# The last batch's first experts: dense after attention, or sparse beside the linear attention

## The chip, the cores and the metric

The kernel runs on one core of one Trainium2 chip. A time is the device time of one execution in microseconds (us); the time of a kernel is the median of its runs. Engines are named as the profile names them: PE (TensorE, matmuls), PEld (its weight loads), DVE (VectorE), ACT (ScalarE), POOL (GpSimd), SP (SyncE, which here issues most transfers). L412 is line 412 of the kernel before.

## What is computed

Four batches of 1024 tokens, each token a row of 128 numbers, pass through four steps, each added to its input:

```python
x = x + attention(x)          # 16 heads of 64, causal, softmax; then @ Wo + bo
x = x + moe(layernorm(x))     # softmax over 32 experts, the best two are used
x = x + linear(layernorm(x))  # 16 heads of 8
x = x + moe(layernorm(x))     # the same experts again
...
def moe(x):                   # expert: a 128x128 matrix
    gates, ids = top_k(softmax(x @ router_w.T), 2)
    return sum(gates[:, j] * (x @ expert_weights[ids[:, j]]) for j in range(2))
...
def linear(x):                # per head; softplus features
    qf = softplus(q) * (sigmoid(g) + 1e-6);  kf = softplus(k)
    kv_cum = cumsum(kf[:, :, None] * v[:, None, :]);  z_cum = cumsum(kf)
    return (qf @ kv_cum) / (qf . z_cum + 1e-6) @ Wo.T
```

The cumulative sums run over the 1024 tokens of a batch. A token's first mixture of experts needs only its own row, so a batch may be in one step while another is in the next.

## The kernel before, in words

All activations stay in one tile `x_sb` of 32 blocks of 128 tokens, eight blocks a batch (`NB = 8`, `NT = 32`). Every step adds into it.

**Attention (L478 to L836).** Its instructions go to the engines in the order in which the code writes them (`tc.manual_schedule()`). For each batch and each pair of heads it goes through eight blocks of queries; `project_out` (L710, L715) multiplies by `Wo` and adds to `x_sb`. At the end of each slot `beside(k)` (L735) runs one or three entries of the list `queue` and one step of the first generator in `sides`.

**Sparse experts, `experts(b, ...)` (L206 to L474).** A generator; each `yield` ends a step. Statistics of eight blocks on DVE (L218); `rstd` and `nb` on POOL (L224); the normed rows on ACT (L240), their transposes on PE, the router's matmul (L248); Exp, the best two, counts (POOL, and PE with a triangle of ones), a list of experts that need another tile (`inc`, `which`) and the place of each token's two rows (`u`, `pos`, `row`). Then come 16 **scatters** (L366): POOL issues an indirect transfer of 128 weighted rows to their places in DRAM and a small memset behind it. The **stream** handles 47 tiles of 128 rows in 12 groups: SP loads rows (L402) and weights (L407, L414), PE transposes (L433), ACT copies (L435), PE multiplies (L422), DVE copies (L427), SP stores (L428). At last 16 **gathers** (L441), indirect transfers issued on POOL: in the first mixture they add straight into `x_sb`; in the second (`came` given) they land in tiles that DVE adds (L468, L473), and SP stores the batch. The scatters and gathers are put into `queue` and run one by one. `passing` lets only one stream run at a time. The small tiles of a run live in a `Room`, and `room.busy` keeps a second run out until the scatters are done.

Before, batches 0, 1 and 2 go through it beside the attention of the batch after each. When attention ends, a loop `while sides or queue` steps until batch 2's gathers are issued.

**Dense experts, `moe(...)` (L849 to L927).** For four blocks at a time (`q`): norm, router, the best two as 32 weights of which 30 are zero; then for each block eight calls of 128x512, four experts each, against all weights held in `we_sb` (L899). Three of eight results are weighted by ACT (L907) and added by POOL (L921 to L924), five are weighted and added by DVE (L914). Its instructions are not in a written order: a scheduler places them. Before, batch 3's first mixture is `moe("f", ...)` (L1043), and so is batch 3's second, `moe("s", ...)` (L1188), at the end of the kernel.

**Linear attention.** `prepare(t, pool)` (L959 to L1034) makes the features of four blocks: statistics (DVE, L966), `rstd` and `nb` (POOL, L971, L974), normed rows (ACT, L980), transposes, projections `pj` (PE, L998), their pieces (ACT, L1002 to L1005), softplus by Exp and Ln (ACT, L1013 to L1021), `ln` and `kq` (POOL, L1027). Before, `prepare(0)` and `prepare(1)` are placed inside the dense stage by `early` (L1036). The constants `tri` (POOL, L944) and `rest` (DVE, L950) stand ahead of it. Then, in a written order again, the loop over blocks `u` (0 to 35, four for the drain): `cumulate` (PE with `tri`, L1077), `products` of the next block (`kv`, POOL, L1059, and a copy on ACT), `outputs` (DVE multiplies the sums with q, L1097), `carry` (PE with `rest`, L1085), `finish` in four steps (L1103 to L1126: a sum, a quotient, a transpose, the output matrix, the residual). Three times in each `u`, `ahead(third)` steps the running `prepare`s (one starts once `12 * started - 26 <= third`) and `beside()` runs one entry of `queue` and one step of every generator of `sides`. The second experts of batches 0, 1 and 2 begin at u = 11, 19 and 27 through `waiting`, in the rooms a, b, a. What is left of them runs between the calls of `moe("s")`.

Of the kernel before, what the change touches and what calls it, by code (L numbers as in the profile page):

```python
# [11 lines left out]
ALU = mybir.AluOpType  # L12
AX = mybir.AxisListType
PSUM = bass.MemoryType.PSUM

P = 128
# [4 lines left out]
def hybrid_kernel(  # L21
# [17 lines left out]
    nc = tc.nc  # L39
    B, N, D = x.shape  # L40
    NB = N // P
    NT = B * NB
# [141 lines left out]
    room = Room(xo, "a")  # L184
# [289 lines left out]
        nc.sync.dma_start(out=out_v[b], in_=x_sb[:, c0 : c0 + NB, :])  # L474


    last = [None]
    with attn as ph:  # L478

        ph.enter_context(tc.manual_schedule())  # L480
# [6 lines left out]
        ps_1 = ph.enter_context(tc.tile_pool(name="ps_1", bufs=3, space=PSUM))  # L487
# [217 lines left out]
        def project_out(b, prs, oTs):  # L705

            for c in range(NB):
                pw = ps_1.tile([P, 512], F32, tag="ps1", name=f"pw_{b}_{c}")
                for i, pr in enumerate(prs):
                    nc.tensor.matmul(  # L710
                        pw[:, :P], oTs[i][:, c * P : (c + 1) * P], wo_sb[:, pr, :],
                        start=(i == 0), stop=(i == len(prs) - 1),
                    )
                xs = x_sb[:, b * NB + c, :]
                last[0] = nc.vector.tensor_tensor(xs, pw[:, :P], xs, ALU.add)  # L715
                yield

        pairs = [(b, pr) for b in range(B) for pr in range(NPAIR)]
# [1 line left out]
        AHEAD = (1, 1, 0, 0, 1, 2, 1, 0)  # L720
# [3 lines left out]
        cur, ahead = project(0, 0)  # L724
# [4 lines left out]
        outs, norms = iter(()), iter(())  # L729
        pend, oTs = None, []  # L730
        HALF = 2
        sides, queue = [], []

        def beside(k):

            for _ in range(3 if k % 2 else 1):
                if queue:
                    queue.pop(0)()
            while sides:
                if next(sides[0], "end") != "end":  # L740
                    break
                sides.pop(0)

        def piece():
            while weighing:
# [50 lines left out]
        for i, (b, pr) in enumerate(pairs):  # L796
            nm = f"{b}_{pr}"
            qT, kT, va = cur
            oT = otp.tile([P, N], F32, tag="oT", name=f"oT_{nm}")
            oTs.append(oT)  # L800
            ahead = iter(())
            if pr == NPAIR - 3 and b + 1 < B:
                norms = normed(b + 1)
            if i + 1 < len(pairs):
                nxt, ahead = project(*pairs[i + 1])
            twos = {}
            for k, ib in enumerate(ORDER):
                two = ib // 2
                if two not in twos:
                    twos[two] = [  # L810
                        ptp.tile([P, 2 * two + 2, 256], F32, tag=f"pT{two}_{h}", name=f"pT_{nm}_{two}_{h}")
                        for h in range(2)
                    ]
                u = Unit(nm, ib, qT, kT, twos[two], ib % 2 * P)
                if k == 5 and pend and pr % HALF == 0:
                    outs = project_out(*pend)
                    pend = None
                if k == 6 and pr == 0 and b > 0:
                    sides.append(experts(b - 1, f"{b - 1}", [ps_1], queue, room))
# [21 lines left out]
    xp = ctx.enter_context(tc.tile_pool(name="xp", bufs=1))  # L841
    came = ctx.enter_context(tc.tile_pool(name="came", bufs=3))
# [87 lines left out]

    lin = ExitStack()
    lw = lin.enter_context(tc.tile_pool(name="lw", bufs=1))
    lb = lin.enter_context(tc.tile_pool(name="lb", bufs=3))
    G = 4
    NE = LD + 1
    PARTS = 3
# [17 lines left out]
    feats = {}  # L957
# [87 lines left out]
    with lin as ph:  # L1045

        ph.enter_context(tc.manual_schedule())
        lp = ph.enter_context(tc.tile_pool(name="lp", bufs=3))
        ps_c = ph.enter_context(tc.tile_pool(name="ps_c", bufs=1, space=PSUM))
        ps_n = ph.enter_context(tc.tile_pool(name="ps_n", bufs=1, space=PSUM))  # L1050
        ps_1 = ph.enter_context(tc.tile_pool(name="ps_l", bufs=4, space=PSUM))
        AHEAD = 26

        def products(u):
# [77 lines left out]
        banks = [ps_1]  # L1132
# [11 lines left out]
        def beside():  # L1144

            if queue:
                queue.pop(0)()
            while waiting and not rooms[waiting[0] % 2].busy:
                b = waiting.pop(0)
                r = rooms[b % 2]  # L1150
                sides.append(experts(b, f"s{b}", banks, queue, r, came))
            for e in list(sides):
                if next(e, "end") == "end":
                    sides.remove(e)

        kv = products(0)
        ends = []
        for u in range(NT + 4):
            if u % NB == 3 and NB < u < NT:
                waiting.append(u // NB - 1)  # L1160
            if u < NT:
                cumulate(u, kv)
                nkv = products(u + 1) if u + 1 < NT else None
                ahead(3 * u)
                m = outputs(u)
            beside()
# [12 lines left out]
            beside()  # L1179

    def rest(pool):

# [40 lines left out]
```

## Time and profile before

| | |
|---|---|
| median of three runs | 2074.32 us (2070.86 to 2074.47) |
| profiled execution, its own time | 2072.33 us |
| its span | 2070.6 us |
| mean granted TensorE clock | 0.953 |
| busy PE / DVE / ACT / POOL | 1846.8 / 1411.0 / 1209.8 / 1168.8 us |
| attention's last matmul, dense stage "f" | 1507.7, then to 1612.4 us |
| first cumulation (u = 0) | 1612.42 us |
| u = 11, u = 16 | 1679.5, 1718.1 us |
| first call of dense "s" | 1876.10 us |

Busy time is the time in which an engine's own instructions run. A line of the timeline gives start, busy time, engine, source line, operation and tiles, and in brackets the idle time of the engine just ahead and what ended it. A line by stretches gives the busy time of each engine in a part of the span; an engine near the stretch's length is its bound, and if none is, the waits tell what it is.

### The profile page before, as it was taken

The page shows a single profiled execution, that of the slowest core. Times are in us where ns is not written, and L with a number is a line of the kernel's source. Part 1 is how long each engine was busy: PE and PEld are TensorE (multiplying, and loading weights), DVE is VectorE, ACT ScalarE, POOL GpSimd, SP SyncE. Part 2 cuts the span into 40 slices and gives each one's busy share as a digit, 9 for nine tenths or more (in the row PEclk, how much of TensorE's full clock was granted, in tenths as well). Part 3 has the DMA queues.
Part 4 walks back from the last instruction along what each step waited for, and adds up shares of the span by engine and source line. Part 5 has one row for each costly group of instructions (what it writes and reads, how often), then busy time and mean ns, then how long its engine had stood idle before and what let it go on. Part 6 is the DMA issues. An engine that isn't in the chain of part 4 may idle for free.

```text
span 2070.6 us, 33623 instructions
## 1 busy us (share of the span) xinstructions
PE 1846.8 (89%) x10100; PEld 1061.6 (51%) x10100; DVE 1411.0 (68%) x4147; ACT 1209.8 (58%) x3777; POOL 1168.8 (56%) x2174
## 2 busy tenths in 40 slices
PE   5999999999999999999999999999668888785765
PEld 2555555555555655555565555556433444463442
DVE  4677776776777677778767778776356677673525
ACT  3766666676676666766666676675345465422312
POOL 3444444444675486457646745683644675967625
PEclk9999999999999999999999999999879998887868
DMA  7000000000003310000231000014210000054651
GB/s 210 1 1 1 1 1 1 1 1 1 1 15 91 92 20 6 1 1 10 67 111 26 11 1 1 3 56 117 45 45 1 1 0 1 18 169 125 191 155 43
DMA packets 151443, 85.22 MB, mean 41 GB/s; under 512 B 8000, under 2 KB 148704, under 8 KB 151136
## 3 DMA queue, kind: packets, MB, share of 16 engines
q1 hardware_dynamic: 139456, 68.91, 11.8%
q0 software_dynamic: 11520, 12.60, 2.8%
q8 instruction: 82, 1.34, 0.3%
q10 hardware_dynamic: 288, 1.57, 0.2%
q14 instruction: 97, 0.79, 0.1%
HBM read 50.02 MB, written 33.03 MB: 40 GB/s over the span
## 4 chain that ended last, share of the span: by engine, by line
PE 61%; ACT 12%; POOL 11%; DVE 10%; issue 4%; SPq 1%; DMA 1%; another core or an unknown queue 1%; ACTq 0%; POOLq 0%; DVEq 0%
PE s L589 18%; PE po L695 10%; PE pt L678 10%; DVE nmx L598 5%; ACT p L623 3%; PE pw L710 3%; PE pk L538 3%; PE pe_f L899 3%; ACT pT L682 2%; POOL x_sb L441 2%; PE cum L1077 2%; PE cum L1085 2%; PE pv L552 2%; PE pe L422 2%; POOL p L665 1%
## 5 line engine op out<-in xcount | busy, mean ns | idle before, releaser
L598 DVE TENSOR_REDUCE nmx<-s 128x2 f32<-128x1024 f32 x512 | 604.5, 1220 | 216.3 <-PE s L589 208.4
L623 ACT ACTIVATE p<-s,nmx 128x512 f32<-128x512 f32 (+3 forms) x640 | 360.7, 575 | 310.1 <-DVE nmx L598 276.7
L589 PE MATMUL s<-kT,qT 64*128 64x512 f32 x2048 | 516.8, 618 | 7.5 <-ACT p L623 4.1
L665 POOL TENSOR_SCALAR p<-p,f,ri 128x512 f32<-128x512 f32 (+3 forms) x768 | 502.8, 670 | 0.7 <-PE s L589 0.4
L678 PEld LDWEIGHTS pt<-ident,p 128*128 128x128 f32 x2304 | 249.3, 141 | 218.0 <-issue 96.6
L678 PE MATMUL pt<-ident,p 128*128 128x128 f32 x2304 | 335.5, 281 | 23.9 <-POOL rs L643 7.0
L682 ACT COPY pT<-pt 128x512 f32<-128x512 f32 (+3 forms) x768 | 323.8, 509 | 13.9 <-PE pt L678 9.5
L647 POOL TENSOR_TENSOR rs<-rs,f 128x2 f32<-128x2 f32 x256 | 51.8, 203 | 438.8 <-ACT f L614 409.3
L695 PE MATMUL po<-pT,va 128*64 128x256 f32 (+1 forms) x2560 | 291.1, 365 | 0.6 <-DVE oT L702 0.6
L589 PEld LDWEIGHTS s<-kT,qT 64*128 64x128 f32 x2048 | 173.0, 185 | 194.8 <-issue 94.9
L628 ACT ACTIVATE p<-s,nmx 128x128 f32<-128x128 f32 x512 | 180.3, 365 | 107.4 <-DVE nmx L598 103.1
L695 PEld LDWEIGHTS po<-pT,va 128*64 128x64 f32 x2560 | 167.0, 136 | 97.2 <-issue 32.4
L636 DVE SCALAR_TENSOR_TENSOR p<-p,qtri 128x128 f32<-128x128 f32 x512 | 145.9, 312 | 6.7 <-ACT p L628 3.3
L643 POOL TENSOR_TENSOR rs<-rs 128x2 f32<-128x2 f32 x192 | 43.8, 228 | 185.7 <-DVE ri L656 185.7
L623 ACT ACTIVATION_READ_ACCUMULATOR p<-s,nmx 128x1 f32 x640 | 138.9, 217 | 0.0
L710 PE MATMUL pw<-wo_sb,oT 128*128 128x128 f32 x512 | 85.5, 292 | 21.9 <-DVE x_sb L715 21.1
L710 PEld LDWEIGHTS pw<-wo_sb,oT 128*128 128x128 f32 x512 | 69.3, 192 | 49.4 <-DVE x_sb L715 21.3
L422 PE MATMUL pe_s<-we_s,xsT_s 128*128 128x128 f32 x282 | 53.0, 333 | 42.7 <-ACT xsT_s L435 20.7
L715 DVE TENSOR_TENSOR x_sb<-pw,x_sb 128x128 f32<-128x128 f32 x128 | 37.1, 290 | 79.3 <-PE pw L710 78.4
L899 PE MATMUL pe_s<-we_sb,xnT_ms 128*128 128x512 f32 x128 | 71.9, 689 | 15.5 <-DVE x_sb L468 5.8
L441 POOL DMA_INDIRECT x_sb<-ys_d,row x48 | 75.8, 1579 | 12.3 <-issue 12.0
L1077 PE MATMUL cum<-kv,tri 128*128 128x384 f32 x192 | 76.1, 537 | 7.2 <-POOL kv L1059 7.0
(330 smaller groups left out, 2764.4 us busy)
## 6 DMA issues: line engine op xcount, KB each, us to landing
xs<-xs_d SPq DMA_DIRECT2D x33, 256.0 KB
ys_d<-ys SPq DMA_DIRECT2D x33, 256.0 KB
xs_s<-xs_d SPq DMA_DIRECT2D x33, 256.0 KB
ys_d<-ys_s SPq DMA_DIRECT2D x33, 256.0 KB
we<-_ffn_expert_weights_dram SPq DMA_DIRECT2D x24, 256.0 KB
we_s<-_ffn_expert_weights_dram SPq DMA_DIRECT2D x24, 256.0 KB
xs_d<-zero SPq DMA_DIRECT2D x2, 3008.0 KB
we<-_ffn_expert_weights_dram SPq DMA_DIRECT2D x45, 64.0 KB
```

What stands on the lines that cost most here:

```text
L589: nc.tensor.matmul(st[:, h, :], self.qT[rows, self.ib * P : (self.ib + 1) * P], self.kT[rows, j * 512 : (j + 1) * 512], start=True, stop=True,
L598: nc.vector.tensor_reduce(self.nmx[:, i, :], self.s[i], AX.X, ALU.max, negate=True)
L623: nc.scalar.activation(self.p[h][:, at : at + m * P], self.s[i][:, h, : m * P], AF.Exp, bias=bias, accum_out=self.rs[:, i, h : h + 1],)
L628: nc.scalar.activation(self.p[h][:, at + m * P : at + (m + 1) * P], self.s[i][:, h, m * P : (m + 1) * P], AF.Exp, bias=bias,)
L636: nc.vector.scalar_tensor_tensor(d, d, 1.0, qtri, ALU.mult, ALU.mult, accum_out=self.rs[:, 2, h : h + 1])
L665: nc.gpsimd.tensor_scalar(w, w, self.f[:, i, h : h + 1], self.ri[:, h : h + 1], ALU.mult, ALU.mult,)
L678: nc.tensor.transpose(pt[:, c * P : (c + 1) * P], self.p[h][:, (g + c) * P : (g + c + 1) * P], ident,)
L682: nc.scalar.copy(self.pTs[h][:, g : g + m, self.col : self.col + P], pt[:, : m * P].rearrange("p (c i) -> p c i", c=m),)
L695: nc.tensor.matmul(po[h * DH : (h + 1) * DH, c0:256], va[:, jb, h, :], pTs[h][:, jb, c0:], start=(jb == 0), stop=(jb == n - 1),)
L710: nc.tensor.matmul(pw[:, :P], oTs[i][:, c * P : (c + 1) * P], wo_sb[:, pr, :], start=(i == 0), stop=(i == len(prs) - 1),)
L899: nc.tensor.matmul(pe, xnT[:, c * P : (c + 1) * P], we_sb[:, 4 * g : 4 * g + 4, :].rearrange("p e d -> p (e d)"), start=True, stop=True,)
L1077: nc.tensor.matmul(sums[i][:, : EP * P], tri, part(kv, i), start=(u % NB == 0), stop=True, skip_group_check=True,)
```

## The change

The last batch's first mixture goes through `experts` too. It is started in the second step of attention's last `project_out`, and there is no loop that drains it: its steps go on inside the linear stage. The dense stage "f" with `early` is gone, and `prepare(0)` and `prepare(1)` are in the written order: 26 calls of `ahead` stand ahead of the first `products`. One `manual_schedule` now reaches from attention's start to the linear loop's end. `beside()` is called inside `ahead()`, three times in each `u`, and more if the features of the next block are not yet there. `prepare(6)`, the first of batch 3, is held until batch 3's experts are done. The rooms change places. The pools that come after attention take `reuse_waits="tile"`: a tile waits for those that used its own memory, not for all of the pool that was there.

```diff
+    order = ExitStack()
+    order.enter_context(tc.manual_schedule())
+    sides, queue = [], []
...
-            while sides:
-                if next(sides[0], "end") != "end":
-                    break
-                sides.pop(0)
+            for e in list(sides):
+                if next(e, "end") == "end":
+                    sides.remove(e)
...
         for _ in project_out(*pend):
+            if k == 1:
+                assert not room.busy
+                sides.append(experts(B - 1, f"{B - 1}", banks, queue, room))
+                final = sides[-1]
             beside(k)
             k += 1
-        while sides or queue:
-            beside(k)
-            k += 1
...
-    late = ctx.enter_context(tc.tile_pool(name="late", bufs=1))
+    late = ctx.enter_context(tc.tile_pool(name="late", bufs=1, reuse_waits="tile"))
...
-    def early(q, pool):
-
-        if q >= NT // 4 - 2:
-            with tc.issue_after(getattr(last[0], "ins", last[0])):
-                for _ in prepare(q - (NT // 4 - 2), pool):
-                    pass
-
-    moe("f", False, NT // 4 - 2, early)
...
-        started, running = 2, []
+        started, running = 0, []
...
+            while waiting and not rooms[(waiting[0] + 1) % 2].busy:
+                b = waiting.pop(0)
+                r = rooms[(b + 1) % 2]
+                sides.append(experts(b, f"s{b}", banks, queue, r, came))
...
             while started < NT // G and 3 * G * started - AHEAD <= third:
+                if G * started // NB == B - 1 and final in sides:
+                    break
                 running.append(prepare(started, ps_1))
                 started += 1
...
+            beside()
+
+        for third in range(-AHEAD, 0):
+            ahead(third)
         kv = products(0)
         ends = []
         for u in range(NT + 4):
+            while u + 1 < NT and (u + 1) // G not in feats:
+                ahead(3 * u)
             if u % NB == 3 and NB < u < NT:
                 waiting.append(u // NB - 1)
             if u < NT:
                 cumulate(u, kv)
                 nkv = products(u + 1) if u + 1 < NT else None
-                ahead(3 * u)
+            ahead(3 * u)
+            if u < NT:
                 m = outputs(u)
-            beside()
...
             ahead(3 * u + 1)
-            beside()
...
             ahead(3 * u + 2)
-            beside()
+    order.close()
```

The same argument stands on the pools `xp`, `came`, `lw`, `lb`, `lp`, `ps_c`, `ps_n` and `ps_l`.

More of the change, by code (lines that the diff above doesn't have):

```diff
@@ L474, in experts @@
         nc.sync.dma_start(out=out_v[b], in_=x_sb[:, c0 : c0 + NB, :])
-    last = [None]
+    order = ExitStack()
+    order.enter_context(tc.manual_schedule())
+    sides, queue = [], []
+    banks = [None]
     with attn as ph:
-        ph.enter_context(tc.manual_schedule())
         xnp = ph.enter_context(tc.tile_pool(name="xnpa", bufs=2))
@@ L714, in project_out @@
                 xs = x_sb[:, b * NB + c, :]
-                last[0] = nc.vector.tensor_tensor(xs, pw[:, :P], xs, ALU.add)
+                nc.vector.tensor_tensor(xs, pw[:, :P], xs, ALU.add)
                 yield
@@ L731, in hybrid_kernel @@
         HALF = 2
-        sides, queue = [], []
+        banks[0] = ps_1
         def beside(k):
@@ L818, in hybrid_kernel @@
                 if k == 6 and pr == 0 and b > 0:
-                    sides.append(experts(b - 1, f"{b - 1}", [ps_1], queue, room))
+                    sides.append(experts(b - 1, f"{b - 1}", banks, queue, room))
                 slot(u, (nm, ib - 1, twos[two], va, oT), k)
@@ L934, in hybrid_kernel @@
     lin = ExitStack()
-    lw = lin.enter_context(tc.tile_pool(name="lw", bufs=1))
-    lb = lin.enter_context(tc.tile_pool(name="lb", bufs=3))
+    lw = lin.enter_context(tc.tile_pool(name="lw", bufs=1, reuse_waits="tile"))
+    lb = lin.enter_context(tc.tile_pool(name="lb", bufs=3, reuse_waits="tile"))
     G = 4
@@ L1034, in prepare @@
         feats[t] = (kq, va)
-    def early(q, pool):
-        if q >= NT // 4 - 2:
-            with tc.issue_after(getattr(last[0], "ins", last[0])):
-                for _ in prepare(q - (NT // 4 - 2), pool):
-                    pass
-    moe("f", False, NT // 4 - 2, early)
-    with lin as ph:
[L1047 to L1051, printed above, removed]
+    with lin as ph:
+        lp = ph.enter_context(tc.tile_pool(name="lp", bufs=3, reuse_waits="tile"))
+        ps_c = ph.enter_context(tc.tile_pool(name="ps_c", bufs=1, space=PSUM, reuse_waits="tile"))
+        ps_n = ph.enter_context(tc.tile_pool(name="ps_n", bufs=1, space=PSUM, reuse_waits="tile"))
+        ps_1 = ph.enter_context(tc.tile_pool(name="ps_l", bufs=4, space=PSUM, reuse_waits="tile"))
         AHEAD = 26
@@ L1127, in finish, with beside @@
             yield
-        started, running = 2, []
+        started, running = 0, []
         waiting = []
         rooms = [room, Room(xp, "b")]
-        banks = [ps_1]
+        banks[0] = ps_1
+        def beside():
+            if queue:
+                queue.pop(0)()
+            while waiting and not rooms[(waiting[0] + 1) % 2].busy:
+                b = waiting.pop(0)
+                r = rooms[(b + 1) % 2]
+                sides.append(experts(b, f"s{b}", banks, queue, r, came))
+            for e in list(sides):
+                if next(e, "end") == "end":
+                    sides.remove(e)
         def ahead(third):
@@ L1142, in ahead @@
                     running.remove(r)
[L1144 to L1154, printed above, removed]
+            beside()
+        for third in range(-AHEAD, 0):
+            ahead(third)
         kv = products(0)
```

4 lines of the change are left out of this document (2 added, 2 removed).

## The prediction

> **What bounds the kernel now.** I read the page's busy shares and 40 slices first. TensorE is busy 97 to 98% of every stretch from 100 us to 1450 us (busy time by stretches), so the attention stage is TensorE's and the change leaves it alone. What the change touches lies after it, so the next view is busy time by stretches, cut where the timeline shows a stage begin: the end of attention, the dense experts "f", u = 0 to 10 of the linear loop, u = 11 to 15, u = 16 to 19, u = 20 to 30, and the tail. The columns are the stretch, its length, busy time with instruction count of PE, PEld, DVE, ACT and POOL, the granted TensorE clock, DMA share and GB/s.
>
> ```profile
> 1474.90:1507.70 32.80, 11.02 (x88) 8.63 (x86) 4.17 (x20) 1.64 (x4) 25.59 (x19) 0.71 0.27 32
> 1507.70:1612.40 104.70, 79.07 (x176) 34.98 (x176) 67.57 (x251) 55.98 (x159) 51.34 (x61) 0.86 0.08 21
> 1612.40:1679.50 67.10, 62.86 (x191) 35.17 (x192) 50.12 (x106) 37.20 (x96) 43.53 (x35) 0.93 0.00 0
> 1679.50:1718.10 38.60, 31.40 (x107) 18.49 (x105) 27.13 (x75) 25.28 (x57) 20.74 (x18) 0.90 0.00 1
> 1760.00:1820.00 60.00, 41.29 (x120) 24.04 (x121) 38.71 (x101) 25.39 (x68) 54.89 (x65) 0.83 0.05 18
> ```
>
> The reader is to see four things. Attention's last 33 us belong to POOL (25.6 of 32.8). The dense stage costs 104.7 us. With nothing beside it the linear loop is TensorE's: 62.86 of 67.10, 94%. Where the experts of another batch run beside it (last line, a part of u = 20 to 30), POOL is what is full: 54.89 of 60, 91.5%.
>
> The timeline shows how the stages hang together (start, busy time, instruction; in brackets the idle time before it and what ended it):
>
> ```profile
> 1502.95 1.56 POOL L441 DMA_INDIRECT x_sb<-ys_d,row  x1 [0.30 <-issue]
> ...
> 1505.13 0.23 DVE L950 TENSOR_SCALAR rest<-tri 128x128 f32<-128x128 f32 x1 [21.59 <-POOL tri L945]
> 1505.61 2.08 PE L710 MATMUL pw<-wo_sb,oT 128*128 128x128 f32 x8 [21.15 <-DVE x_sb L715]
> 1511.39 1.65 ACT L980 ACTIVATE xn_l<-x_sb,nb_l,rstd_l 128x128 f32<-128x128 f32 x4 [34.85 <-POOL nb_l L974]
> 1514.24 6.31 PE L998 MATMUL pj<-wc,xnT_l 128*128 128x512 f32 x8 [0.67 <-ACT xnT_l L988]
> ...
> 1612.42 4.21 PE L1077 MATMUL cum<-kv,tri 128*128 128x384 f32 x6 [5.70 <-POOL kv L1059]
> ```
>
> DVE stands 21.6 us at `rest`, which waits for POOL's `tri`, which is queued behind 16 gathers of batch 2; the last begins at 1502.95. POOL is free at 1504.5.
>
> **The change, part by part.** The base is the profiled execution, 2072.3 us (span 2070.6 and 1.7 around it), 2.0 under the median shown, 2074.3.
>
> *1. Out: the dense stage; in: a lead-in.* The first cumulation moves from 1612.4 to the time when POOL and ACT have made the first features. In the changed order the last residual adds stand ahead of `rest`, so PE's 21 us stall goes; what is late next is POOL, still in its gathers until 1504.5, because the first step of both new chains (`rstd` of the experts and of `prepare(0)`) is queued behind them. So I gain nothing there. From 1504.5:
> - constants, room memsets, `rstd` of both chains (1.7 and 2.3 us): until about 1512.6.
> - ACT, in order: eight `xn` of the experts and four of `prepare(0)` (12 x 0.48), three transposed copies (0.6 each), the projection's rows (6.3 on PE at its low clock, with the copies beside it), then 1.12 and 1.04 (Exp, `u`), two table loads of 1.28, 0.63, 1.06, the experts' Exp and copies: about 21.3, so 1533.9.
> - POOL: four `ln`/`kq` rows of 1.27 = 5.1, counts 3.2, `gt` 1.3, `inc` 2.6, `u` 3.8, `pos` 2.3, the next `rstd` 1.7, `kv` 2.1, and some 2.5 of DVE and PE answers between them: 24.6, so 1558.
> That is **-54**. The bounds: only POOL's own sum behind 1512.6, ACT wholly beside it, 1536.5: -76; the chains beside each other worse by 10: -44. The weights' load for the dense stage is issued in both and is needed only at the tail, 300 us later. Waiting by tile I cost at nothing: the first work of the later pools begins at 1511.39 after 34.85 us, and POOL's `nb` ended that wait, not a bank; if a bank did, the price is inside the -44.
>
> *2. In: the scatters and the stream, beside u = 0 to 10.* The group of matmuls of a stream that ran beside the linear loop, u = 28 on:
>
> ```profile
> L422 PE MATMUL pe_s<-we_s,xsT_s 128*128 128x128 f32 x94 | 15.6, 305 | 3.1 <-DMA we_s<-_ffn_expert_weights_dram 2.1 <-ACT xsT_s L435 0.6
> L433 PE MATMUL pxs_s<-ident,xs_s 128*128 128x128 f32 x47 | 7.6, 286 | 0.1
> ```
>
> 23.2 us of PE (its records can be a few per cent short). PE was the bound there at 94%, so (62.9 + 23.2)/0.94 = 91.6 for 67.1: **+24.5**. POOL would have 43.5 + 16 scatters of 1.26 (0.96 and the memset with its gap) = 20.2 + 5.1 of routing left = 68.8, under 91.6, so the scatters hide; they are +20.2 more, +45, if each delays `kv`. The lower bound is +10: PE and its weight loads wait at `cum` for POOL's `kv` (6.0 and 8.3 us, overlapping) and for other things there, and some of the matmuls fall into such waits. Weight loads and rows come by SP's queue, whose DMA share there was 0.00, and which nothing of the loop uses. ACT (37 + 12) and DVE (50 + 8) stay below.
>
> *3. In: 16 accumulating gathers, at u = 11 to 15.*
>
> ```profile
> L366 POOL DMA_INDIRECT xs_d<-xw_s,row_s x48: 952/959/1347, 1776.2 to 1944.1; - x48
> L441 POOL DMA_INDIRECT x_sb<-ys_d,row x16: 1554/1558/1622, 1474.9 to 1502.9; - x16
> ```
>
> (minimum, median and maximum in ns.) By the start times one gather takes 1.86 us with its gap; 16 are 29.8. POOL then has 20.7 + 29.8 = 50.5 in a stretch of 38.6, so it takes PE's place as the bound: at the 91.5% of the last stretch above it is 55.2, **+16.6**. Bounds: 0, if `kv` runs ahead and the loop drains it; +23.7 at 81%, POOL's share over all of u = 20 to 30. A check from another row: u = 20 to 30 ran at 8.9 us each beside experts, so u = 0 to 15 at that pace is 142 for 105.7, +36, against my 41.1.
>
> *The rule that speaks against it.* Both kinds of indirect DMA are written on POOL, while DVE is 70 to 75% busy. The Trainium skill, "SBUF — State Buffer", section "A bandwidth-pool intuition that's wrong (but worth ruling out)", holds that such a DMA of about 620 ns takes about 3100 ns beside a DVE copy, since GpSimd cannot write its descriptors while DVE holds the port they share. By that page, an estimate, the 32 would grow by 16 x 2.14 + 16 x 1.54 = 59 us and the change would lose. The scatters above, the first of them beside a DVE that was 65% busy (1760 to 1820), have a median of 959 and a maximum of 1347 ns, and the row goes into my sum.
>
> *4. u = 16 to 35.* The same steps in the same order; `prepare(6)`, held until the last batch's experts are done, comes at u = 16, and its features are needed at u = 24: 0, or one block's 8 us if the experts end four blocks late.
>
> *5. The tail.* In the changed order eight dense calls that stood ahead of batch 1's stream stand inside it and eight others move into batch 2's; the last 32 come after the last stream in both. The work is the same: **+2**, from -8 to +10 (the first eight took 9.7 us).
>
> *Sum.* -54 + 24.5 + 16.6 + 2 = -10.9: 2061.4 on the base, **2061**.
>
> **The rivals.**
> - *Hidden work* (about 2035). PE's matmuls fall into its waits and POOL's gathers run while `kv` is three blocks ahead: half of 24.5 and a third of 16.6 remain, so -54 + 12.3 + 5.5 + 0 = -36. For it: the loop's waits at `cum` reach 5.7 and 6.5 us, which other matmuls can fill, and `kv` has three buffers. Against it: 1760 to 1820, where the same kind of mix ran at 8.9 us a block.
> - *No change* (2070 to 2078). The lead-in is the long one, -44, and the loop's price stays 43. For it: a dozen handovers between POOL, ACT and DVE in which any queue can stand on the wrong chain. Against it: the sum above already has both chains one after the other on POOL.
> - *Slower* (about 2095). One mechanism: POOL is in order, `kv` (2.1 us) is queued behind indirect DMAs, and each of the 32 holds up the chain from `kv` to `cum` by its whole length: 16 x 1.26 + 16 x 1.86 = 50 us, on top of the stream's 24.5 and the tail's 2: 76.5 against 54, +22.5. It decides once u = 0 to 15 lasts over 105.7 + 54 = 160 us, 10 us a block. For it: the longest waits of `cum` in that stretch are for `kv` (6.5 and 5.7 us). Against it: 8.9 a block with 32 such DMAs beside u = 20 to 30.
> - That the change does not do what it says: if the experts' chain fell so late that its scatters began only with u = 11, nothing would be lost in the first stretch, but batch 0's second experts and `prepare(6)` would wait; that lands in the no-change case.
>
> **How the numbers follow.** 0.2% of the time, 4.1 us, is about what a measurement of this kernel can tell from no change. The chances: forecast (2047 to 2070) 0.40, hidden work (below 2047) 0.18, no change (2070 to 2078) 0.13, slower 0.29. So faster 0.58, same 0.13, slower 0.29. The range leaves out the best half of the hidden case (under 2034, where the lead-in's -76 would lie) and the upper end of the slower one: 2034 to 2092. The forecast's own range is 2047 to 2070.
>
> **What would show it.** First cumulation at about 1558 (1: below 1550 or above 1568 is wrong). u = 11 at about 1650 and a PE share over 90% before it (2: if POOL is fuller than PE there, the slower rival's mechanism works). u = 16 at about 1705 with POOL over 90% between (3). The last cumulation some 13 us earlier than before's, and the tail's length from there within 10 us of before's (4, 5). Indirect DMAs whose median is over 2 us would make the page's rule right and my rows wrong. A wait of `cum` for `kv` that sums to over 30 us in u = 0 to 15 would show the slower rival.

## The result and the profile after

The changed kernel takes 2079.8 us (median of 13 runs, 2076.59 to 2087.13), the kernel before, run beside it, 2070.86 (13 runs): **1.0039** of before, 95% interval 1.0028 to 1.0049. It is slower by 8 to 9 us. The forecast was 2061, and faster at 0.58; it moved the other way. The profiled execution has a span of 2078.1 for 2070.6, and the 7.5 us between them are what is to be explained.

The same view as in the prediction, busy time by stretches (stretch, length, busy time and count of PE, PEld, DVE, ACT, POOL, granted clock, DMA share, GB/s), for the changed kernel: the lead-in, u = 0 to 5, 6 and 7, 8 to 10, 11 to 15, 16 to 19, 20 to 30, and all that follows.

```profile
1510.00:1565.80 55.80, 21.95 (x52) 10.78 (x52) 13.46 (x58) 35.02 (x81) 29.46 (x47) 0.62 0.00 1
1565.80:1610.30 44.50, 38.17 (x107) 20.39 (x108) 29.55 (x56) 21.79 (x59) 38.66 (x46) 0.90 0.06 21
1610.30:1636.90 26.60, 18.35 (x92) 13.83 (x92) 10.60 (x22) 12.51 (x24) 10.34 (x9) 0.81 0.59 166
1636.90:1670.20 33.30, 27.56 (x137) 18.70 (x136) 18.35 (x39) 14.71 (x38) 16.29 (x13) 1.00 0.53 151
1670.20:1717.80 47.60, 31.67 (x106) 17.94 (x105) 26.79 (x71) 23.61 (x55) 39.05 (x31) 0.86 0.14 17
1717.80:1759.80 42.00, 30.17 (x79) 16.34 (x79) 28.13 (x89) 15.95 (x40) 32.10 (x31) 0.84 0.05 7
1759.80:1860.40 100.60, 79.58 (x314) 50.91 (x313) 69.23 (x182) 40.35 (x103) 82.36 (x108) 0.88 0.28 81
1860.40:2078.10 217.70, 141.84 (x505) 86.50 (x503) 99.19 (x314) 56.77 (x167) 121.12 (x162) 0.72 0.46 130
```

The kernel before, in stretches that the prediction did not cut so fine: u = 0 to 5, u = 6 to 10, and all behind u = 31.

```profile
1612.40:1650.20 37.80, 36.39 (x108) 20.17 (x109) 26.26 (x58) 18.37 (x49) 22.91 (x19) 0.92 0.00 0
1650.20:1679.50 29.30, 26.47 (x85) 15.00 (x84) 23.86 (x48) 18.82 (x47) 20.62 (x17) 0.94 0.00 1
...
1849.10:2070.60 221.50, 140.74 (x519) 87.55 (x517) 99.19 (x316) 60.11 (x174) 123.65 (x168) 0.78 0.46 130
```

| stretch | before | after | difference |
|---|---|---|---|
| to the first cumulation | 1612.4 | 1565.8 | -46.6 |
| u = 0 to 5 | 37.8 | 44.5 | +6.7 |
| u = 6 to 10 | 29.3 | 59.9 | +30.6 |
| u = 11 to 15 | 38.6 | 47.6 | +9.0 |
| u = 16 to 19 | 33.4 | 42.0 | +8.6 |
| u = 20 to 30 | 97.6 | 100.6 | +3.0 |
| behind u = 31 | 221.5 | 217.7 | -3.8 |

The reader is to see that no engine is full where most of it is lost: in the third line of the first fence TensorE is busy for 18.35 of 26.60 us and POOL for 10.34, and the DMA share is 0.59. The timeline there:

```profile
1614.63 0.96 POOL L366 DMA_INDIRECT xs_d<-xw,row  x1 [0.18 <-issue]
...
1617.00 0.92 SPq L402 DMA_DIRECT2D xs<-xs_d  x2
...
1619.88 1.09 PE L433 MATMUL pxs<-ident,xs 128*128 128x128 f32 x4 [6.60 <-DMA xs<-xs_d]
```

The last scatter goes out at 1614.6, SP can issue the stream's first load only after it (the waits of SP's queue give `L402 <- DMA xs_d<-xw,row` 7.5 us), and TensorE, whose next work in order is the transposes of those rows, stands 6.6 us. The cumulation of u = 7 is queued behind and comes at 1629.0, 18.6 us after that of u = 6; between the two in the kernel before lie 5.1.

### The profile page after: what moved, and what is told of

Same layout as the page of the kernel before. It is cut to its first block, busy times and chain, and to the rows that moved or that the text cites. A ratio compares the mean times of both kernels' runs of the same rounds, so it can differ in the third digit from the quotient of the medians.

```text
span 2078.1 us, 33646 instructions
## 1 busy us (share of the span) xinstructions
PE 1816.7 (87%) x10117; PEld 1056.7 (51%) x10117; DVE 1368.5 (66%) x3983; ACT 1200.5 (58%) x3721; POOL 1203.1 (58%) x2216
## 5 line engine op out<-in xcount | busy, mean ns | idle before, releaser
L441 POOL DMA_INDIRECT x_sb<-ys_d,row x64 | 102.6, 1604 | 16.5 <-issue 16.4
L711 PEld LDWEIGHTS pw<-wo_sb,oT 128*128 128x128 f32 x512 | 68.6, 190 | 27.9 <-ACT pT L683 12.7
```

What stands on the lines that cost most here:

```text
L441: g_.indirect_dma_start(to, None, yd, bass.IndirectOffsetOnAxis(ap=row[:, j, c : c + 1], axis=0), **how)
L711: nc.tensor.matmul(pw[:, :P], oTs[i][:, c * P : (c + 1) * P], wo_sb[:, pr, :], start=(i == 0), stop=(i == len(prs) - 1),)
```

## The experiments

Each set of runs was on one chip, with runs of the kernel before; their medians were 2072.4, 2069.8, 2061.6, 2062.7 and 2073.1 us (the second and the fourth set on a chip of the same number). So times are compared as ratios to the kernel before of the same set (changed kernel: 1.0039). Stretches up to u = 31 are compared directly: the changed kernel, run again in the last set, agreed with its first profile within 0.5 us in each of them. In the cuts of code, `...` marks what is left out.

**The price in parts.** Three runs leave out a part of the last batch's first experts.

```diff
 # e1_no_stream
-        groups = [(g, min(4, NTILE - g)) for g in range(0, NTILE, 4)]
+        groups = [(g, min(4, NTILE - g)) for g in range(0, NTILE, 4) if nm != "3"]
 # e2_no_indirect
-                f(*a, **k)
+                if nm != "3":
+                    f(*a, **k)
 # e6_no_gather
-                f(*a, **k)
+                if nm != "3" or f is scatter:
+                    f(*a, **k)
```

Expected of e1_no_stream:

> Leaves out the stream of the last batch's first experts (its loads, transposes, matmuls, copies and stores); the scatters and gathers stay, so the output is not the reference's. In the changed kernel u = 0 to 10 took 104.4 us where the kernel before took 67.1. Theory A (the stream costs by waits for transfers that stand in TensorE's queue, not by its matmuls' time): u = 0 to 10 falls to about 74, by 30 us, clearly more than the 23 us of its matmuls, and the whole time falls to about 2050. Theory B (TensorE's work): it falls by 23 to 25, to about 80. Theory C (POOL's indirect transfers in front of kv): it falls by under 12, to over 92.

Expected of e2_no_indirect:

> Leaves out the 16 scatters and 16 gathers (with the small memsets) of the last batch's first experts; the stream stays, on old rows, so the output is not the reference's. Theory A: u = 0 to 5 (44.5 us, before 37.8) gets some 7 us back, the stretch with the stream keeps its length (u = 6 to 10 about 60), u = 11 to 15 gets 9 and u = 16 to 19 gets 8 to 9 back: the time falls by about 25, to 2055. Theory C (each delays kv by its whole length): it falls by 50, to 2030. Theory B: it falls by under 10.

Expected of e6_no_gather:

> Leaves out only the 16 gathers of the last batch's first experts, so the output is not the reference's; with the run that left out scatters and gathers (27 us faster than the changed kernel) it splits their price. If the scatters cost what the stretches of that run suggest (6.7 us at u = 0 to 5 and 7.9 at u = 6 to 10, where POOL was 92.6% busy): 15 us of the 29 are the gathers', the time is about 2065, and u = 0 to 10 stays at 104 us. If the gathers are all of it: 2051. If the scatters are all of it: no change, 2079.

Measured: 0.9892 (0.987 to 0.9915), 0.9902 (0.9879 to 0.9926) and 0.9985 (0.9974 to 0.9995); spans 2050.2, 2048.7 and 2064.6. By the spans the stream costs 27.9 us, the gathers 13.5, the scatters the difference of the last two, 15.9 (by the ratios 30, 11 and 17, each uncertain by some 3 to 5 us, since the intervals of two ratios come together there). Together 57.3, and the loop from the first cumulation to u = 31 was 57.9 longer. u = 0 to 5 and u = 6 to 10 without the indirect transfers:

```profile
1566.20:1604.00 37.80, 35.91 (x107) 20.15 (x108) 26.97 (x56) 21.54 (x59) 25.08 (x19) 0.92 0.00 0
1604.00:1656.00 52.00, 43.26 (x225) 30.37 (x224) 30.82 (x60) 27.57 (x61) 22.07 (x17) 1.00 0.54 153
```

The first 37.8 us are those of the kernel before, and POOL's 25.08 stand beside 38.66 of the changed kernel. So 13.6 us of POOL lengthen these six blocks by 6.7. Another 7.9 lie in u = 6 to 10 (52.0 for 59.9), where TensorE stands 6.6 us for the scattered rows in the changed kernel. u = 11 to 15 without the gathers took 38.4 us (before 38.6, changed 47.6), so they cost 9 there. Without the stream u = 0 to 10 fell by 17 us, not by A's 30, since the gathers then came into this stretch (from 1622.0 on); the whole fell by 28, to the 2050 that A named. Without the indirect transfers A named 25 and C 50 us; it was 29. B's 23 to 25 us are near the stream's 27.9 in size, but it has nothing for the scatters, and the next runs show that not all of the stream's price is work.

**Waits of the stream.** Three runs look at whether the stream costs by waits or by work.

```diff
 # e4_far (also: row tiles 3 -> 4, result tiles 2 -> 3)
+        far = 1 if nm == "3" else 0
...
-            if 0 <= i - 2 < len(groups):
-                g, n = groups[i - 2]
+            if 0 <= i - 2 - far < len(groups):
+                g, n = groups[i - 2 - far]
 # e10_moves
-            if 0 <= i - 3:
+            if 0 <= i - 3 and nm != "3":
...
+                if nm == "3":
+                    nc.sync.dma_start(out=yv[:, g : g + n, :], in_=xs[g][:, :n, :])
+                    yield
+                    continue
 # e11_work
+                xs[g] = xn[:, g % 8 : g % 8 + 4, :]
...
+                    wts[g] = we_sb[:, g % 32 : g % 32 + 4, :]
...
-                nc.sync.dma_start(out=yv[:, g : g + n, :], in_=ys[:, :n, :])
+                if nm != "3":
+                    nc.sync.dma_start(out=yv[:, g : g + n, :], in_=ys[:, :n, :])
```

Expected of e4_far:

> The same work; only in the last batch's first stream, rows are loaded one step earlier than they are used (four row tiles for three, three result tiles for two; the two larger rings hold for all streams). Theory A: the waits for rows (6.6 us) and for the stores of results (9.9 us) in u = 6 to 10 go in good part: that stretch falls from 60 by 8 to 15 us and the time to about 2068. Theory B and theory C: no change, within 3 us.

Expected of e10_moves:

> In the last batch's first stream only the transfers stay (rows, weights, and a store of the unchanged rows); its transposes, matmuls and copies are left out, so the output is not the reference's. Without the stream the time was 2051, with it 2080. If the stream costs by its work on TensorE, ACT and DVE, this is near 2052 and u = 6 to 10 near 43 us. If it costs by its transfers (SP's queue, the row and weight transfers, a later start of the gathers), this is near 2075.

Expected of e11_work:

> The counterpart: the same transposes, matmuls and copies in the same places, but on rows and weights that already lie in SBUF, and nothing is loaded or stored, so the output is not the reference's. If the stream costs by its work, near 2077. If it costs by waits for its transfers in TensorE's queue, near 2055, and u = 6 to 10 falls from 60 us to below 50.

Measured: 1.0034 (1.0022 to 1.0045), 1.0069 (1.005 to 1.0088) and 0.9986 (0.9975 to 0.9996). e4 gave nothing: u = 6 to 10 took 59.0 for 59.9. e11 gave 12.7 of the 60 us (u = 6 to 10: 47.2) and put the first gather at 1656.0 instead of 1670.8; the whole gain is some 11 us. So some 11 of the stream's 28 us are its transfers and 17 its work, and one step more of distance does not hide them. e10 is no clean test of the transfers, because its stores hold the row tiles and SP stood 27.2 us for them; but what it does to the loop is plain. Its waits between 1644 and 1690 (engine, line, what it waited for; us in all, times, longest):

```profile
ACT xn_l L984 <- POOL nb_l L978: 36.8, 1, 36.8
POOL x_sb L445 <- DMA ys_d<-xs: 36.7, 1, 36.7
PEld pxn_l L991 <- ACT xn_l L984: 33.6, 4, 33.0
PE pxn_l L991 <- ACT xn_l L984: 31.8, 1, 31.8
```

With no work of the stream in TensorE's queue the loop ran on to u = 12 at 1644.4, and then stood 44 us: POOL's first gather waits for the stream's last store, the features' `nb` is queued behind it on POOL, ACT waits for `nb`, TensorE for ACT. The time won in the loop is handed back at the gather.

**The start of the lead-in.**

```diff
 # e5_hold
+        while nm == "2" and not over[0]:
+            yield
...
 # e7_early, e8_before_early (beside takes that many steps)
...
-            beside(k)
+            beside(k, 2 if k in (0, 4) else 1)
 # e12_ahead
-        AHEAD = 26
+        AHEAD = 22
```

Expected of e5_hold:

> The same work; the 16 gathers of batch 2 are held until attention is over, so that they stand among the steps of the lead-in and not ahead of all of them on POOL (they are due at u = 15). If POOL's queue at attention's end sets the start of the lead-in, the first cumulation comes at about 1555 instead of 1565.8 (18 us gained at the start, some 8 lost to the gathers in between) and the time falls by 5 to 12, to about 2070. If the lead-in's own chain over ACT sets it, or the gathers cost there what they cost before, first cumulation within 3 us of 1565.8.

Expected of e7_early:

> The changed kernel with one edit in attention: in two of eight slots the running experts make two steps instead of one, so that batch 2's gathers fall inside attention, where TensorE is the bound, and POOL is free when attention ends. If those gathers set the start of the lead-in, the first cumulation comes 14 to 17 us earlier, at about 1550, and the time is about 2064. If the lead-in's own chain sets it, or the gathers then slow attention, within 4 us of 2080.

Expected of e8_before_early:

> The kernel before with the same edit in attention. There rest waits for tri behind the same gathers (21.6 us of DVE, 21.15 of TensorE): if that wait is on its path, the first cumulation comes about 18 us earlier and the time is about 2053; if the features' chain inside the dense stage covers it, under 5 us earlier. The first would say that the kernel before had more to gain at this place than the changed one.

Expected of e12_ahead:

> The same work with a lead-in of 22 rounds for 26, so that fewer steps of the second features and of the experts stand ahead of the first kv on POOL. My lead-in came out at 61 us for 53.5, and in the order POOL stood 5.6 us for the second features' projection. If those steps are the 7.4 us, the first cumulation comes at 1558 or earlier; the time falls by the same only if the loop does not pay for them. I expect first cumulation 6 to 9 us earlier, and the total within 4 us of 2080, since POOL is full in u = 0 to 5.

Measured: 1.0033 (1.0018 to 1.0049), 1.0054 (1.0035 to 1.0073), 0.9997 (0.9985 to 1.0009) and 1.0103 (1.0085 to 1.012). In e5 the lead-in's first `rstd` came at 1492.0 instead of 1508.9, and the first cumulation still at 1567.4: the 16 gathers cost as much between its steps as ahead of them (from that `rstd` to the last step of the first features, 37.4 us in the changed kernel, it took 56.0).

In e7 batch 2's gathers were done within attention, from 1433.1 to the last at 1479.5, and attention ended 22.8 us later. That is not the price of these gathers, since the edit works on the experts of every batch and attention was late before. TensorE's first scores of batch 2, of batch 3, and the last output projection, of the changed kernel and then of e7:

```profile
734.84 1.56 PE L590 MATMUL s<-kT,qT 64*128 64x512 f32 x6
1105.39 1.56 PE L590 MATMUL s<-kT,qT 64*128 64x512 f32 x6
...
1482.66 4.03 PE L711 MATMUL pw<-wo_sb,oT 128*128 128x128 f32 x32
```
```profile
743.86 1.56 PE L590 MATMUL s<-kT,qT 64*128 64x512 f32 x6
1121.77 1.56 PE L590 MATMUL s<-kT,qT 64*128 64x512 f32 x6
...
1505.44 4.03 PE L711 MATMUL pw<-wo_sb,oT 128*128 128x128 f32 x32
```

So e7 is 9.0 us late when batch 2 begins, 16.4 when batch 3 begins, and 22.8 at the end. Only the first of the three stretches holds 16 gathers more than in the changed kernel (batch 0's, from 681.7 on); the other two have as many in both, one batch's for another's, and still get 7.4 and 6.4 us longer. What the edit does to attention besides is open. Behind attention e7 gains: from the last scores to the first cumulation it takes 81.8 us for 100.5. The gathers do set the start of the lead-in, as the prediction had it, and attention takes the gain back. e8 shows the same of the kernel before: the last scores come 25.5 us later, the way from there to the first cumulation is 23.3 shorter (123.9 for 147.2), and the first cumulation stays (1614.6 for 1612.4). The 21 us wait at `rest` is on the path, but was not to be had by this edit.

e12 put the first cumulation at 1556.5, 9 us earlier, and u = 0 to 10 then took 116.3 for 104.4, so u = 11 came at 1672.8 for 1670.2: nothing was kept. More was lost later. u = 31 came at 1879.0 for 1860.4, and by its ratio e12 is some 13 us slower than the changed kernel, where no loss was expected; these runs do not show why.

**The end of the chain.** The gathers' cost, the hold on `prepare(6)`, and the wait at u = 7.

```diff
 # e9_plain: the gathers land in tiles, DVE adds
+        to = came or (lands[0] if nm == "3" else None)
+        if to is None:
...
 # e13_half: e9, and
...
+                if G * started // NB == B - 1 and final in sides and (
+                    len(halves) < 2 or G * started % NB
+                ):
 # e14_no_hold
-                if G * started // NB == B - 1 and final in sides:
-                    break
 # e18_gap: ahead of the stream's first step
+        for _ in range(3 if nm == "3" else 0):
+            yield
```

Expected of e9_plain:

> The changed kernel, but the last batch's 16 first gathers don't accumulate: they land in tiles and four DVE additions add them, as in the second mixture (0.95 us each instead of 1.56). If POOL's queue is the bound at u = 11 to 18, 16 times 0.6 is some 9 us less there, 2071; if the count of handovers matters and not POOL's time, within 3 us of 2080.

Expected of e13_half:

> The same work as the reference's: the last batch's first gathers don't accumulate (as in the run before that kept 2080 although u = 11 to 19 got 11.5 us shorter), and the features of block 24 begin once the first half of the batch is added, not after all of it. If the late start of those features is what ate the 11.5 us (u = 20 to 30 took 121.5 instead of 100.7), that stretch falls back to about 101 and the time to about 2068. If it was something else, 2080.

Expected of e14_no_hold:

> The features of block 24 on are started when the loop is due for them and not held until the last batch's experts are done, so they read some rows before the experts are added, and the output is not the reference's. If the chain from the scatters to these features paces u = 16 to 23 (they began at 1730.8, due at about 1710), that stretch gets 8 to 12 us shorter and the time is about 2070. If POOL's queue alone does it, no change, 2080.

Expected of e18_gap:

> The same work; three steps of the loop (one block) stand between the last scatter and the stream's first transposes in TensorE's order, so that the first rows have landed when TensorE comes to them. If that wait is a price of its own, u = 6 to 10 gets 5 to 7 us shorter and the time falls by as much, to 0.997 of the changed kernel's. If the chain through the gathers sets the pace, u = 7 gets faster and the rest slower by the same, and the time stays within 2 us.

Expected of c_after:

> The changed kernel unaltered, for the comparison on one chip: 1.0039 of the kernel before; first cumulation at 1565 and 294 us from there to u = 31 as in its first profile. If chips differ in the tail alone, its tail differs from 217.6 by as much as the kernel before differs from its 2070.9.

Measured: 1.0042 (1.0026 to 1.0059), 1.0029 (1.0018 to 1.0041), 1.0044 (1.0027 to 1.0061), 1.0029 (1.0017 to 1.004) and, for the changed kernel, 1.0032 (1.002 to 1.0045). None separates from the changed kernel. e9, e13 and e18 made the stretch shorter that they aimed at: e9 u = 11 to 19 (78.0 us for 89.6, given back at u = 20 to 30, 121.5 for 100.6), e13 u = 20 to 30 (97.8), e18 u = 6 to 10. e14 did so in part: u = 16 to 19 fell to 34.5 for 42.0, but u = 16 to 23, at which it aimed, took 75.3 for 74.7. (In e14 the rows that `prepare(6)` reads had been added by then: the twelfth gather went out at 1715.2, its `rstd` at 1722.9.) e18, u = 6 to 10, u = 20 to 30 and all behind u = 31:

```profile
1611.90:1662.40 50.50, 42.47 (x220) 29.87 (x220) 29.28 (x61) 27.32 (x60) 26.70 (x22) 1.00 0.59 168
...
1750.60:1878.80 128.20, 90.71 (x348) 58.12 (x347) 72.12 (x186) 51.31 (x130) 94.03 (x127) 0.83 0.29 85
1878.80:2077.50 198.70, 129.45 (x474) 80.05 (x472) 96.19 (x311) 52.42 (x153) 113.06 (x147) 0.77 0.45 128
```

The stretch with the stream is 9.7 us shorter than 60.2 of the changed kernel on the same chip, its clock 1.00, and u = 20 is reached at 1750.6 for 1760.4. Then the loop stands for the features of block 24, which came at 1786.4 for 1782.0, and the end is 2077.5 for 2081.2. Lay the runs side by side by that event, the DVE instruction that finishes these features; in the changed kernel and in the kernel before it is

```profile
1781.34 1.74 DVE L1033 SCALAR_TENSOR_TENSOR kq<-gt,kq 128x512 f32<-128x512 f32 x1 [1.35 <-POOL kq L1028]
```
```profile
1771.11 0.69 DVE L1033 SCALAR_TENSOR_TENSOR kq<-gt,kq 128x512 f32<-128x512 f32 x1
```

| kernel | first cumulation | u = 20 | features of block 24 | span | span less features |
|---|---|---|---|---|---|
| before | 1612.4 | 1751.5 | 1771.1 | 2070.6 | 299.5 |
| after | 1565.8 | 1759.8 | 1781.3 | 2078.1 | 296.8 |
| e12_ahead | 1556.5 | 1756.7 | 1781.7 | 2077.5 | 295.8 |
| e9_plain | 1564.9 | 1748.4 | 1784.2 | 2080.1 | 295.9 |
| e18_gap | 1567.5 | 1750.6 | 1786.4 | 2077.5 | 291.1 |
| e6_no_gather | 1566.5 | 1747.6 | 1770.0 | 2064.6 | 294.6 |
| e2_no_indirect | 1566.2 | 1730.4 | 1752.8 | 2048.7 | 295.9 |
| e1_no_stream | 1566.2 | 1729.8 | 1750.8 | 2050.2 | 299.4 |

The span follows neither the first cumulation nor u = 20. In these eight profiles it ends 291 to 300 us after the features of block 24. (In the runs that are not in the table it is 288 to 301 us, and 284 in e16_all and e17_before_resident, which are told next.)

That the end hangs on this event is not shown, and three runs speak against it. e13 has these features at 1773.5 and e14 at 1777.1, 7.8 and 4.2 us before the changed kernel, and neither time separates from it; e12 has them where the changed kernel has them, and is 13 us slower. The table hides this, as its spans come from sets that differ by up to 11.5 us in the kernel before. With each ratio times 2070.9, less the 1.8 us around the span, in place of the span, the distance is 289 to 302 us in these and the other runs without e16 and e17, and 309 in e12. Neighbouring events fit as well: in the same reckoning the cumulation of u = 24 lies 277 to 287 us before the end in all 18 profiles other than e16's and e17's, e12's among them.

**Fewer transfers.** Here the first 32 tiles of a stream take their weights from `we_sb`.

```diff
+                here = g < E and nm == "3"     # e15; in e16 and e17 all streams behind attention
+                if here:
+                    wts[g] = we_sb[:, g : g + 4, :]
```

Expected of e15_resident:

> The same work; the last batch's first stream takes the weights of its first 32 tiles from the copy of all weights that already lies in SBUF for the last dense stage, so eight of its transfers of 256 KB go. If the transfers pace the stream (some 56 us for 12 groups), the first gather comes 8 to 15 us earlier than 56 us after the last scatter, u = 6 to 10 falls from 60 to about 50, and the time is about 2070. If TensorE's work or the row transfers (scatter, load, store, gather one behind the other) pace it, within 3 us of 2080.

Expected of e16_all:

> The same work: the edits of the run with the first half's features (gathers that don't accumulate), and resident weights in the last batch's first stream and in all three second streams. If the transfers pace the streams beside the loop and in the tail (DMA share there 0.5 to 0.66), the tail after u = 31 gets 10 to 25 us shorter too, and the time is below that of the kernel before, about 0.985 of it. If the rows' transfers pace them, about 1.000.

Expected of e17_before_resident:

> The kernel before, with resident weights in its three second streams and nothing else. If the tail is paced by weight transfers, 10 to 25 us faster than before, about 0.99. If not, the same within 3 us.

Measured: 1.0031 (1.0018 to 1.0043), 0.9968 (0.9957 to 0.9978) and 0.9961 (0.9949 to 0.9974). In the first stream weights are not what it waits for: u = 6 to 10 took 58.2. In the three second streams they cost something: without them the kernel before is 8 us faster, less than the 10 to 25 expected. e16 and e17 beat both kernels, and they don't differ by more than their intervals: with the weights resident the change is worth nothing, with e13's edits beside it.

## Why the prediction was wrong

**The step that failed** is step 2's "so the scatters hide". The scatters were priced at nothing because POOL's 68.8 us fit under TensorE's 91.6 in u = 0 to 10. But the scatters all lie ahead of 1615.6, in u = 0 to 6, and the stream's matmuls all behind them, since the stream reads what they wrote. POOL is full in the first part while TensorE has only the loop:

```profile
1565.80:1593.10 27.30, 23.57 (x67) 13.08 (x68) 19.98 (x35) 11.32 (x36) 25.27 (x28) 0.89 0.07 22
```

That is 25.27 of 27.30 us, 92.6%. Then TensorE has the stream, while POOL is busy for 26.6 of 59.9 us. Two loads of one dependent chain were laid on top of each other in a sum over both parts. They come one after the other, and the scatters cost 15.9 us, where the forecast had 0. That is most of the 18.4 us between forecast and result; the lead-in's 7.4 come next.

Step by step, forecast and measured:

| step | forecast | measured |
|---|---|---|
| 1 lead-in | -54 (-76 to -44) | -46.6 |
| 2 stream | +24.5 | +27.9 |
| 2 scatters | 0 | +15.9 |
| 3 gathers | +16.6 | +13.5 |
| 4, 5 remaining loop and tail | +2 | -3.2 (rest of 7.5) |
| sum | -10.9 | +7.5 |

*Step 1* had the right mechanism. POOL stayed in its gathers to the 1504.0 that were forecast as 1504.5, and the first `rstd` came at 1508.9. It is 7.4 us too good, inside its bounds: in the written order the second features' projection stands there too, and POOL's `gt` waits 5.58 us for it at 1549.2. By e12 it would not have mattered, because the 9 us won there were lost again by u = 11. (One bound was added up wrong: 24.6 us behind 1512.6 is 1537.2, not 1536.5.)

*Step 2, the stream*, is right within 3.4 us, but not for the reason given. By e11 some 17 us are work and some 11 are transfers and the wait for them; 23.2 us of matmuls at 94% was near by luck. TensorE was not the bound: it was busy for 84.1 of the 104.4 us of u = 0 to 10, 80.5%, where the forecast asked for over 90, and u = 11 came at 1670.2, not at 1650.

*Step 3* is right in its sum and its engine, not in its place: POOL is 39.05 of 47.60 us busy, 82% and not 91.5%, and e6 gives back 9.2 us in that stretch and 4.2 in the next.

*Step 4* priced the end of the chain at 0 "or one block's 8 us if the experts end four blocks late". They ended at u = 17 (last gather 1725.7), `rstd` of `prepare(6)` began at 1730.8 (1720.2 in the kernel before), and u = 16 to 19 took 8.6 us more, of which e6 gives back 4.2; the table counts that with the gathers. The sum never looked at the last batch as one chain from attention's end to block 24, whose links come one after the other: routing (to 1563), scatters (1568 to 1615.6), stream (1617 to 1668), gathers (1670.8 to 1727.3), features (1730.8 to 1781.3). In the kernel before the dense stage took that chain's place and the features were ready at 1771.1. The prices of scatters, stream and gathers are measured by e1, e2 and e6. That the last link, the wait for the features, costs time of its own is not shown: e13 and e14 made it shorter, and the time stayed.

*The rivals.* The slower one (2095, 0.29) names POOL's indirect transfers; it is nearest in sign. Its size was 50 us for the 32, measured were 29.4: they cost 0.9 us each, not their whole 1.26 and 1.86. Its mechanism, `kv` held up in POOL's queue, is not what the waits show: apart from the one ahead of u = 0, TensorE's waits of `cum` for `kv` in u = 0 to 15 add up to 3.9 us, where the prediction named 30 as the sign. What the prediction held against it was misread, though: beside u = 20 to 30 the kernel before has 17 indirect transfers, not 32. Its point of decision, u = 0 to 15 longer than 105.7 + 54 = 160 us, was not reached: they took 152.0. With the lead-in's real 46.6 that point is 152.3, so up to u = 16 the change was even, and the 8.6 us of u = 16 to 19 are as much as the loss. Hidden work did not come: stream and scatters cost more than was forecast, and the gathers only 3.1 us less.

*The rule of the skill.* The last batch's 16 scatters took 958, 1008 and 1449 ns (minimum, median, maximum), its gathers 1540, 1564 and 2392, beside a DVE that was 66% and 56% busy in those stretches. The Trainium skill, "SBUF — State Buffer", section "A bandwidth-pool intuition that's wrong (but worth ruling out)", has 3100 ns for such a transfer beside a DVE copy. No transfer here came to that, and the rule's 59 us did not come, though the kernel is slower as it would have said. In both stretches DVE ran multiplications, sums, statistics and the like, and no copy, so the page's own case did not arise and is not refuted.

What stays open: what the end of the kernel hangs on. Its distance from the features of block 24, and from u = 24, varies by some 10 us in most kernels, whatever lies before, but the two runs that brought the features of block 24 forward without leaving work out (e13, e14) did not clearly move the end. That the three second streams pace the part behind it is suggested by e16 and e17 (284 us in both, with fewer weight transfers), not shown for each stream.

## What to carry to other kernels

Where a sparse path takes the place of a dense stage, write its links down as one chain (route, scatter, stream, gather, and the step that waits for it) with the time at which the result is due, and compare that with the kernel before, ahead of any sum of busy times: work on two engines hides under each other only if neither waits for the other. A step that makes the loop start earlier, or a stretch shorter, is worth only what is left of it at the end: e12 won 9 us at the start, e9 11.6 and e18 9.7 in the loop, and none was faster. Laying many kernels side by side tells which events keep their distance from the end, not which of them sets it; for that an event has to be moved alone. And where an edit works on every repetition of a stage, compare the start of each repetition before a delay is put down to the last one.

## What the runs showed of the hardware that was not expected

In u = 11 to 17 sixteen accumulating gathers took 1.54, 1.56 and 2.39 us (minimum, median, maximum); in e9, in the same places, gathers that don't accumulate took 0.94, 0.99 and 1.44 us. The median of one kernel differs by 11.5 us between sets of runs (2061.6 and 2073.1 for the kernel before), and by 7.1 between two sets on a chip of the same number (2069.8 and 2062.7), so it is open what the chip has to do with it. The changed kernel's profile has 217.7 us behind u = 31 in one set and 219.8 in another, against 210.4 to 214.6 of five kernels with the same work there (e10, e11, e13, e14, e15) on the two faster sets, while the stretches before agree in the changed kernel's two profiles. This hints that the difference lies in the part with the many transfers; as u = 31 comes at other times in other kernels (198.7 us behind it in e18, in the set whose kernel before took longest), it is not shown.
